# First attention's front: norms per token, a diagonal product to spread them, roots as powers on GpSimd, and first rows read by tile

## The chip, the cores and the metric

The kernel runs on one core of one Trainium2 chip, as a single launch. Its time is the device time of one execution in microseconds (us). Eleven executions of the kernel before gave a median of 2311.44 us, from 2306.51 to 2316.15. One further execution was recorded by the profiler; all profile lines come from that one.

The engines are named as in the profile: PE is TensorE (matmuls; PEld is its weight loads), DVE is VectorE, ACT is ScalarE, POOL is GpSimd, SP is SyncE, whose queue issues most DMAs.

## The reference

The input x has 2708 rows (tokens) of 256 features, with an adjacency matrix of 2708 x 2708. Four layers follow, each an attention over the graph and a feed-forward part. Only the front of the first attention is changed:

```python
def _L0_gnn_ref(features, adj, Wq, Wk):
    def _cos_normalize(x):
        n = jnp.linalg.norm(x, axis=-1, keepdims=True)
        return x / jnp.maximum(n, COS_EPS)          # COS_EPS = 1e-4
    Qn = _cos_normalize(features @ Wq.T)
    Kn = _cos_normalize(features @ Wk.T)
    raw_att = Kn @ Qn.T
    att = jnp.where(adj > 0, raw_att, NEG) * TEMP
    att = jax.nn.softmax(att, axis=1)
    prop_fea = att @ features
...
x = x + _L0_gnn_ref(_layernorm(x, axis=-1), adj, L0_gnn_Wq, L0_gnn_Wk)
```

So every token is layernormed, projected to a query and a key of 128 numbers each, both are divided by their lengths, and the scores are products of these unit vectors.

## The kernel before

The tokens lie in 22 tiles of 128 (the last holds 20) and are worked on in six chunks of 512 (the last has 148): chunk 0 is tiles 0 to 3, and so on. `K.__init__` has `load_x` (L65) read all rows, one DMA for a chunk (L72), each but the first two waiting until the one two before has landed.

`fast_l0_gnn` (L1690) computes the first attention. Its `front` (L1721) prepares one chunk:

1. `norm_chunk` (L1633): mean and variance of each tile on DVE (L1642, L1643), then 1/sqrt(variance + 1e-5) as a square root on ACT (L1645) and a reciprocal on DVE (L1646), a shift (L1647), and the scaling of the tiles into `fa`, the odd ones on ACT (L1654), the even ones on DVE (L1656).
2. Eight PE transposes (L1625) and two copies give the features by rows, `fT` (L100 on DVE, L102 on ACT).
3. Eight matmul instructions (L1732; every f32 product of this kernel appears as two) give Q and K, transposed: 128 features by 512 tokens. ACT squares each into `sq` (L1740), DVE copies each to `QT` and `KT` (L1741).
4. Norms. For Q, the squares of 128 tokens at a time are the weights against a column of ones (L1747): a column of sums with a token on each partition, `rq`, which the exponential later takes as its scale. For K the norm must lie along the free axis, in every partition: a matrix of ones times the squares (L1754) gives a 128x512 tile of sums.
5. Square roots of both on ACT (L1758, L1762), maximum with 1e-4 and reciprocal on DVE (L1767, L1768 for Q; L1770, L1771 for K, over 128x512), and on POOL the product of `KT` with the result (L1773).

Then the scores: for each chunk g of targets and each tile j of sources a step (`scores`, L1804): one product of `QT` and `KT` (L1811), Exp on ACT with the scale `rq` (L1835), the mask by the adjacency tile on DVE (L1836), and, two steps later (`sums`, L1850), four products with `fa` that accumulate (L1867). Six chunks by 22 tiles make 132 steps.

The front of chunk 0 is written ahead of the loop. The fronts of chunks 1 to 5, some rows for the last tile and weights of the next layer (`fronts`, L1781) are a generator, of which the loop takes two pieces per step during the first 22 steps. Tile j of the sources needs `QT`, `rq` and `fa` of its own chunk; the scores of chunk g need the whole `KT` of that chunk. The fronts share two PSUM tiles (`psf`, L1715).

Engines run their instructions strictly in the order of their queues. That order is made when the kernel is built: a planner simulates the program with estimated durations and gives an engine, when it is free, the earliest written instruction that is ready by the estimate. It may thus put work of a later chunk ahead of an instruction of chunk 0 that still waits. `issue_after(ins)` makes the instructions written inside it come behind `ins` on that engine's queue. The waits themselves are semaphores that the framework sets by the data.

Of the kernel before, what the change touches and what calls it, by code (L numbers as in the profile page):

```python
# [8 lines left out]
F32 = mybir.dt.float32  # L9
# [4 lines left out]
AF = mybir.ActivationFunctionType  # L14
# [31 lines left out]
class K:  # L46
# [3 lines left out]
    def __init__(self, ctx, tc, x_in):  # L50
        self.tc = tc
        self.nc = nc = tc.nc
        self.flip = 0
        pool = ctx.enter_context(tc.tile_pool(name="shared", bufs=1))
        self.x = pool.tile([128, NT, D], F32, name="x")
        nc.vector.memset(self.x[:, NT - 1, :], 0.0)
        self.load_x(lambda r: x_in[r])
        self.ident = pool.tile([128, 128], F32, name="ident")
        make_identity(nc, self.ident)
        self.ones = pool.tile([1, 128], F32, name="ones")  # L60
        nc.vector.memset(self.ones, 1.0)
        self.eps = pool.tile([128, 1], F32, name="eps")
        nc.vector.memset(self.eps, 1e-5)

    def load_x(self, src, also=None):  # L65


        ld = []
        for c0, cs in CHUNKS:
            t0, n = c0 // 128, cs // 128  # L70
            ld.append(
                self.nc.sync.dma_start(  # L72
                    self.x[:, t0 : t0 + n, :],
                    src(slice(c0, c0 + n * 128)).rearrange("(t p) d -> p t d", p=128),
                )
            )
            if cs % 128:
                ld.append(
                    self.nc.sync.dma_start(
                        self.x[:TAIL, NT - 1, :], src(slice((NT - 1) * 128, N))  # L80
                    )
                )
        for i, inst in enumerate(ld):
            if also:
                also(inst)
            if i > 1:
                self.tc.add_manual_dep(
                    inst.ins,
                    ld[i - 2].ins.name,
                    mybir.DependencyInfo(  # L90
                        mybir.DependencyClass.Sync, mybir.DependencyReason.DATA
                    ),
                    reason="the first are to land first",
                )
# [1433 lines left out]
class Fast(K):  # L1528
# [101 lines left out]
            dst = out(kk)  # L1630
            self.copy(dst, p[:, : dst.shape[-1]])

    def norm_chunk(self, pool, fa, t0, n, spare=False):  # L1633


        nc = self.nc
# [5 lines left out]
            nc.vector.bn_stats(st, self.x[:, t0 + i, :])  # L1642
            nc.vector.bn_aggr(mv[:, i, :], st)  # L1643
        yield
        nc.scalar.activation(rs[:, :n], mv[:, :n, 1], AF.Sqrt, bias=self.eps)  # L1645
        nc.vector.reciprocal(rs[:, :n], rs[:, :n])  # L1646
        nc.vector.scalar_tensor_tensor(  # L1647
            sh[:, :n], mv[:, :n, 0], -1.0, rs[:, :n], ALU.mult, ALU.mult
        )
        for i in range(n):  # L1650
            src, dst = self.x[:, t0 + i, :], fa[:, i, :]
            r, s = rs[:, i : i + 1], sh[:, i : i + 1]
            if i % 2 or spare:
                nc.scalar.activation(dst, src, AF.Identity, bias=s, scale=r)  # L1654
            else:
                nc.vector.tensor_scalar(dst, src, r, s, ALU.mult, ALU.add)  # L1656
        yield

    def logits(self, fa, fT, dst, wg, bg, E, pool):
# [30 lines left out]
def fast_l0_gnn(k, adjT, wqkT, pool_, other):  # L1690
# [7 lines left out]
    with ExitStack() as ctx:  # L1698
# [19 lines left out]
        def psum():  # L1718
            return psf.tile([128, 512], F32, name="f_ps")

        def front(c0, cs):  # L1721
            bl = blocks(c0, cs)
            t0, n = bl[0][0], len(bl)
            yield from k.norm_chunk(two, fa[:, t0:, :D], t0, n)
            fT = two.tile([128, 2, 512], F32, name="fT")
            k.transposed(fa, bl, psum, lambda kk: fT[:, kk, :cs])
            yield
# [14 lines left out]
                q.append(sq)  # L1742
            yield

            pq, pk = psum(), psum()
            for t, o, m in bl:
                nc.tensor.matmul(  # L1747
                    pq[:m, t - t0 : t - t0 + 1],
                    lhsT=q[0][:, o : o + m],
                    rhs=every[:, :1],  # L1750
                    start=True,
                    stop=True,
                )
            nc.tensor.matmul(pk[:, :cs], lhsT=every, rhs=q[1][:, :cs], start=True, stop=True)  # L1754
            for m in sorted({b[2] for b in bl}):
                ts = [b[0] for b in bl if b[2] == m]
                r = slice(ts[0], ts[-1] + 1)
                nc.scalar.activation(  # L1758
                    rq[:m, r], pq[:m, ts[0] - t0 : ts[-1] + 1 - t0], AF.Sqrt
                )  # L1760
            rk = one.tile([128, 512], F32, name="rk")
            nc.scalar.activation(rk[:, :cs], pk[:, :cs], AF.Sqrt)  # L1762
            yield
            for m in sorted({b[2] for b in bl}):
                ts = [b[0] for b in bl if b[2] == m]
                r = rq[:m, ts[0] : ts[-1] + 1]
                nc.vector.tensor_scalar(r, r, 1e-4, None, ALU.max)  # L1767
                nc.vector.reciprocal(r, r)  # L1768
            r = rk[:, :cs]
            nc.vector.tensor_scalar(r, r, 1e-4, None, ALU.max)  # L1770
            nc.vector.reciprocal(r, r)  # L1771
            kt = KT[:, c0 : c0 + cs]
            nc.gpsimd.tensor_tensor(kt, kt, r, ALU.mult)  # L1773
            yield

        def last_rows():
# [134 lines left out]
        side = fronts()  # L1911
        todo = [(g, j) for g in range(G) for j in range(NT)]
        ahead = []
        for i in range(len(todo) + 2):
            if i < len(todo):
                ahead.append(scores(*todo[i]))
# [3164 lines left out]
```

## Time and profile before

| | |
|---|---|
| median of 11 executions | 2311.44 us (2306.51 to 2316.15) |
| the profiled execution, its own time | 2316.39 us |
| its span, first to last instruction | 2314.7 us |
| mean granted PE clock | 0.954 (1.00 in the first 300 us) |
| first transpose (L1625) | 9.28 us |
| first projection (L1732) | 11.92 us |
| first score (L1811) | 26.30 us |
| first and last sum (L1867) | 30.7 and 373.9 us |
| ACT table loads of the first attention's chunk 0, from 26 to 112 us | 13, each 1283 ns |
| reciprocal over 128x512 (L1771) | 5, each 3351 ns |

The profile is read in four views. The page gives each engine's busy time and a row of 40 slices with the busy share in tenths. The view by stretches gives the busy time of each engine in a part of the span. The waits say who waited for whom, how long in total, how often, and the longest. The timeline lists instructions in order: start, duration, engine, line, operation, output <- inputs, shape, count, and in brackets the idle time before and what ended it. A duration of several merged instructions reaches from the first's start to the last's end, and a matmul's contains the time in the pipeline; how fast PE goes is read from the starts.

### The profile page before, as it was taken

To read this page: it belongs to the slowest core of one execution; us is meant where nothing else is said; L and a number is where in the kernel's file an instruction comes from. 1 tells how busy PE (TensorE), PEld (TensorE's weight loads), DVE (VectorE), ACT (ScalarE), POOL (GpSimd) and SP (SyncE) were. 2 spreads that over 40 slices of the span, in tenths; PEclk is the share of its full clock that TensorE was granted. 3 is DMA by queue.
4 is the path that set the end of the run, shared out by engine and by line. 5 is a ranking of instruction groups with operands and counts; after the bars stand their busy time and mean duration, and the time that the engine had idled before them with its cause. 6 is when DMAs were issued, how large, how long until landed. Compare 5 with 4: busy or idle time off the path is not lost. (4 is left out here: it accounts for less than half of the span.)

```text
span 2314.7 us, 31484 instructions
## 1 busy us (share of the span) xinstructions
PE 2151.8 (93%) x11216; PEld 1486.0 (64%) x11216; DVE 1491.7 (64%) x3382; ACT 694.5 (30%) x1501; POOL 477.3 (21%) x558
## 2 busy tenths in 40 slices
PE   7999999989999999999799999689999999986997
PEld 4766675568898767777578877457743333335885
DVE  7478887846695287467646563163588898872544
ACT  7556554221112222122230013023551221211221
POOL 2000002202353333664200012314110000003221
PEclk9999999979999999999899996899999999997998
DMA  5244323021497242441355544012133333415440
GB/s 151 66 112 114 110 78 113 1 78 49 142 255 216 75 117 67 100 94 22 81 160 150 143 136 98 3 40 86 49 92 97 114 115 91 123 42 183 142 144 15
DMA packets 167888, 235.28 MB, mean 102 GB/s; under 512 B 31901, under 2 KB 101251, under 8 KB 167716
## 3 DMA queue, kind: packets, MB, share of 16 engines
q1 hardware_dynamic: 112176, 154.91, 23.1%
q0 software_dynamic: 36592, 62.13, 10.8%
q10 hardware_dynamic: 18948, 16.05, 2.2%
q8 instruction: 95, 1.56, 0.3%
q14 instruction: 77, 0.63, 0.1%
HBM read 200.31 MB, written 33.22 MB: 101 GB/s over the span
## 5 line engine op out<-in xcount | busy, mean ns | idle before, releaser
L3583 DVE SCALAR_TENSOR_TENSOR PT<-Rr,Q,aj 128x512 f32<-128x512 f32 (+3 forms) x630 | 395.6, 681 | 104.9 <-PE acc_ps L3682 80.5
L3757 PE MATMUL acc_ps<-PT,V 128*64 128x512 f32 (+4 forms) x2016 | 333.7, 551 | 0.0
L3757 PEld LDWEIGHTS acc_ps<-PT,V 128*64 128x64 f32 (+1 forms) x2016 | 94.2, 123 | 210.3 <-issue 159.6
L1867 PE MATMUL acc_ps<-fa,PT 128*128 128x257 f32 x882 | 215.1, 383 | 1.2 <-DVE out L1887 1.2
L1867 PEld LDWEIGHTS acc_ps<-fa,PT 128*128 128x128 f32 x882 | 163.9, 190 | 67.3 <-issue 35.4
L3682 PE MATMUL acc_ps<-V,PT 128*128 128x257 f32 x882 | 196.6, 384 | 2.0 <-issue 1.9
L3682 PEld LDWEIGHTS acc_ps<-V,PT 128*128 128x128 f32 x882 | 167.8, 192 | 29.7 <-issue 2.8
L3340 PE MATMUL y_ps<-w2t,hT 128*128 128x256 f32 x768 | 173.6, 384 | 0.1
L3323 PE MATMUL h_ps<-xT,w1t 128*128 128x384 f32 (+2 forms) x544 | 168.7, 466 | 1.5 <-ACT hT L3330 1.3
L3340 PEld LDWEIGHTS y_ps<-w2t,hT 128*128 128x128 f32 x768 | 146.2, 193 | 20.9 <-DVE wgat L3807 0.5
L3323 PEld LDWEIGHTS h_ps<-xT,w1t 128*128 128x128 f32 x544 | 103.0, 199 | 54.3 <-ACT xT L3312 3.3
L3330 ACT ACTIVATE hT<-h_ps,b1t 128x384 f32<-128x384 f32 (+2 forms) x136 | 73.2, 539 | 179.3 <-PE h_ps L3323 176.9
L3354 POOL DMA_INDIRECT acc<-ys,ids x48 | 91.8, 1913 | 153.5 <-DVE ys L3351 104.1
L2538 PE MATMUL acc_ps<-V,at 128*128 128x258 f32 (+3 forms) x924 | 119.0, 286 | 2.3 <-DMA at<-in_adjT 1.6
L1811 PE MATMUL s_ps<-KT,QT 128*128 128x512 f32 (+1 forms) x252 | 116.4, 548 | 3.7 <-ACT PT L1835 2.3
L4784 POOL DMA_INDIRECT xe<-fd,idg x32 | 32.8, 1023 | 418.1 <-DVE ids L4754 401.9
L1836 DVE SCALAR_TENSOR_TENSOR PT<-aj,PT 128x512 f32<-128x512 int32 (+1 forms) x126 | 79.1, 632 | 56.8 <-ACT PT L1835 56.5
L2538 PEld LDWEIGHTS acc_ps<-V,at 128*128 128x128 f32 (+1 forms) x924 | 111.8, 185 | 5.5 <-DMA at<-in_adjT 2.5
L4310 PE MATMUL y_ps<-w2t,hT 128*128 128x256 f32 (+1 forms) x432 | 103.9, 390 | 6.8 <-issue 6.8
L1791 ACT ACTIVATE junk<-aj,mhalf 128x512 bf16<-128x512 int32 (+1 forms) x126 | 84.3, 669 | 77.4 <-DMA aj<-in_adjT 76.6
L3348 DVE TENSOR_TENSOR ys<-y_ps,b2t 128x256 f32<-128x256 f32 x48 | 20.3, 422 | 128.3 <-PE y_ps L3340 91.1
L4310 PEld LDWEIGHTS y_ps<-w2t,hT 128*128 128x128 f32 (+1 forms) x432 | 80.3, 191 | 24.1 <-issue 10.8
(800 smaller groups left out, 3526.3 us busy)
## 6 DMA issues: line engine op xcount, KB each, us to landing
aj<-in_adjT SPq DMA_DIRECT2D x294, 256.0 KB, 2.6
at<-in_adjT POOLq DMA_DIRECT2D x105, 256.0 KB
w1t<-in_L_ffn_W SPq DMA_DIRECT2D x8, 1024.0 KB
w2t<-in_L_ffn_W SPq DMA_DIRECT2D x8, 1024.0 KB, 6.3
w1t<-in_L_ffn_w SPq DMA_DIRECT2D x8, 1024.0 KB
w2t<-in_L_ffn_w SPq DMA_DIRECT2D x8, 1024.0 KB, 5.7
fd<-fa ACTq DMA_DIRECT2D x13, 512.0 KB, 3.3
aj<-in_adjT SPq DMA_DIRECT2D x21, 202.0 KB, 2.6
```

What stands on the lines that cost most here:

```text
L1791: nc.scalar.activation(junk, src, AF.Square, bias=k.mhalf, accum_out=dst)
L1811: nc.tensor.matmul(s[:, :cs], lhsT=QT[:, j * 128 : j * 128 + 128], rhs=KT[:, c0 : c0 + cs], start=True, stop=True,)
L1836: made[0] = nc.vector.scalar_tensor_tensor(PT[p, :n], aj[p, :n], 0.0, PT[p, :n], ALU.is_gt, ALU.mult)
L1867: nc.tensor.matmul(ac, lhsT=PT[:, o : o + n], rhs=fa[:, j, :], start=j == 0, stop=False)
L2538: nc.tensor.matmul(ac[:n, :c], lhsT=at[:, o : o + n], rhs=V[:, j, r], start=j == 0 and q == 0, stop=False, skip_group_check=True,)
L3323: nc.tensor.matmul(hp, lhsT=w1t[:, kk, m * 128 : (m + 1) * 128], rhs=self.xT[:, kk, cs], start=(kk == 0), stop=(kk == 1),)
L3340: nc.tensor.matmul(y, lhsT=self.hT[:, m, i * 128 : (i + 1) * 128], rhs=w2t[:, m, :], start=(m == 0), stop=(m == M - 1),)
L3354: add = nc.gpsimd.indirect_dma_start(out=acc, out_offset=bass.IndirectOffsetOnAxis(ap=self.ids[:, i : i + 1], axis=0), in_=ys, in_offset=None,
L3583: nc.vector.scalar_tensor_tensor(PT, R, Q, aj, ALU.max, ALU.mult)
L3682: nc.tensor.matmul(ac[:n], lhsT=PT[:, o : o + n], rhs=V[:, j, 0, :], start=(j == 0), stop=False,)
L3757: nc.tensor.matmul(w.pop("out"), **w)
L4310: last = nc.tensor.matmul(y[:n], lhsT=hT[:, m, o : o + n], rhs=wts[e][1][:, m, :], start=(m == 0), stop=(m == M - 1),)
```

## The change

- `load_x` can read chunk 0 with a DMA for each of its four tiles, and does so at the start of the kernel. The later reads wait as before for the read two before them (chunk 2 for tile 3).
- The first piece of the following fronts, the statistics of chunk 1, is taken right behind chunk 0's front and tied with `issue_after` to the last DVE instruction that normalises chunk 0.
- Where `power` is set (chunks 1 to 5), `norm_chunk` adds 1e-5 on DVE and raises to -1/2 on POOL; ACT's root and DVE's reciprocal go. Chunk 0 keeps them.
- The norms of K come as those of Q do, a column per 128 tokens with a token on each partition; both lie in one PSUM tile, eight columns. The lower bound is applied to the squared length (1e-8); then root and reciprocal (chunk 0) or a power on POOL (the others), over at most eight columns. `rq` is a copy of the first four.
- To spread K's factors along the free axis, DVE makes four diagonal blocks, the identity times the factors (128x512), and a matrix of ones times these gives them in every partition. DVE instead of POOL multiplies `KT` with that, out of PSUM.
- In chunk 0 an Exp of one column, whose result nobody reads, follows the root on ACT.

```diff
@@ -54,7 +54,7 @@
         pool = ctx.enter_context(tc.tile_pool(name="shared", bufs=1))
         self.x = pool.tile([128, NT, D], F32, name="x")
         nc.vector.memset(self.x[:, NT - 1, :], 0.0)
-        self.load_x(lambda r: x_in[r])
+        self.load_x(lambda r: x_in[r], tiles=True)
         self.ident = pool.tile([128, 128], F32, name="ident")
         make_identity(nc, self.ident)
         self.ones = pool.tile([1, 128], F32, name="ones")
@@ -62,12 +62,21 @@
         self.eps = pool.tile([128, 1], F32, name="eps")
         nc.vector.memset(self.eps, 1e-5)
-    def load_x(self, src, also=None):
-        ld = []
+    def load_x(self, src, also=None, tiles=False):
+        ld, free = [], 2
         for c0, cs in CHUNKS:
             t0, n = c0 // 128, cs // 128
+            if tiles and c0 == 0:
+                for t in range(n):
+                    ld.append(
+                        self.nc.sync.dma_start(
+                            self.x[:, t, :], src(slice(t * 128, t * 128 + 128))
+                        )
+                    )
+                free = n + 1
+                continue
             ld.append(
                 self.nc.sync.dma_start(
                     self.x[:, t0 : t0 + n, :],
@@ -83,7 +92,7 @@
         for i, inst in enumerate(ld):
             if also:
                 also(inst)
-            if i > 1:
+            if i >= free:
                 self.tc.add_manual_dep(
                     inst.ins,
                     ld[i - 2].ins.name,
@@ -1630,7 +1639,7 @@
             dst = out(kk)
             self.copy(dst, p[:, : dst.shape[-1]])
-    def norm_chunk(self, pool, fa, t0, n, spare=False):
+    def norm_chunk(self, pool, fa, t0, n, spare=False, power=False):
         nc = self.nc
@@ -1642,8 +1651,13 @@
             nc.vector.bn_stats(st, self.x[:, t0 + i, :])
             nc.vector.bn_aggr(mv[:, i, :], st)
         yield
-        nc.scalar.activation(rs[:, :n], mv[:, :n, 1], AF.Sqrt, bias=self.eps)
-        nc.vector.reciprocal(rs[:, :n], rs[:, :n])
+        if power:
+            nc.vector.tensor_scalar(rs[:, :n], mv[:, :n, 1], 1e-5, None, ALU.add)
+            half = self.mhalf.to_broadcast([128, n])
+            nc.gpsimd.tensor_tensor(rs[:, :n], rs[:, :n], half, ALU.pow)
+        else:
+            nc.scalar.activation(rs[:, :n], mv[:, :n, 1], AF.Sqrt, bias=self.eps)
+            nc.vector.reciprocal(rs[:, :n], rs[:, :n])
         nc.vector.scalar_tensor_tensor(
             sh[:, :n], mv[:, :n, 0], -1.0, rs[:, :n], ALU.mult, ALU.mult
         )
@@ -1653,7 +1667,9 @@
             if i % 2 or spare:
                 nc.scalar.activation(dst, src, AF.Identity, bias=s, scale=r)
             else:
-                nc.vector.tensor_scalar(dst, src, r, s, ALU.mult, ALU.add)
+                self.normed = nc.vector.tensor_scalar(
+                    dst, src, r, s, ALU.mult, ALU.add
+                )
         yield
     def logits(self, fa, fT, dst, wg, bg, E, pool):
@@ -1721,7 +1737,7 @@
         def front(c0, cs):
             bl = blocks(c0, cs)
             t0, n = bl[0][0], len(bl)
-            yield from k.norm_chunk(two, fa[:, t0:, :D], t0, n)
+            yield from k.norm_chunk(two, fa[:, t0:, :D], t0, n, power=c0 > 0)
             fT = two.tile([128, 2, 512], F32, name="fT")
             k.transposed(fa, bl, psum, lambda kk: fT[:, kk, :cs])
             yield
@@ -1742,35 +1758,58 @@
                 q.append(sq)
             yield
-            pq, pk = psum(), psum()
-            for t, o, m in bl:
+            pn = psum()
+            for s in (1, 0):
+                for t, o, m in bl:
+                    nc.tensor.matmul(
+                        pn[:m, 4 * s + t - t0 : 4 * s + t - t0 + 1],
+                        lhsT=q[s][:, o : o + m],
+                        rhs=every[:, :1],
+                        start=True,
+                        stop=True,
+                    )
+            rn = two.tile([128, 2, 4], F32, name="rn")
+            for m in sorted({b[2] for b in bl}):
+                ts = [b[0] - t0 for b in bl if b[2] == m]
+                r = slice(ts[0], ts[-1] + 1)
+                v = rn[:m, :, r]
+                nc.vector.tensor_scalar(
+                    v,
+                    pn[:m, :8].rearrange("p (s t) -> p s t", s=2)[:, :, r],
+                    1e-8,
+                    None,
+                    ALU.max,
+                )
+                if c0 == 0:
+                    nc.scalar.activation(v, v, AF.Sqrt)
+                    nc.vector.reciprocal(v, v)
+                else:
+                    half = k.mhalf[:m, :, None].to_broadcast([m, 2, len(ts)])
+                    nc.gpsimd.tensor_tensor(v, v, half, ALU.pow)
+                nc.vector.tensor_copy(rq[:m, t0 + r.start : t0 + r.stop], v[:, 0, :])
+            if c0 == 0:
+                nc.scalar.activation(rn[:, 0, 0:1], rn[:, 0, 0:1], AF.Exp, scale=0.0)
+            yield
+            dg = one.tile([128, 4, 128], F32, name="dg")
+            pk = psum()
+            for m in sorted({b[2] for b in bl}, reverse=True):
+                ts = [b[0] - t0 for b in bl if b[2] == m]
+                r, n = slice(ts[0], ts[-1] + 1), len(ts)
+                nc.vector.tensor_tensor(
+                    dg[:m, r, :m],
+                    k.ident[:m, None, :m].to_broadcast([m, n, m]),
+                    rn[:m, 1, r, None].to_broadcast([m, n, m]),
+                    ALU.mult,
+                )
                 nc.tensor.matmul(
-                    pq[:m, t - t0 : t - t0 + 1],
-                    lhsT=q[0][:, o : o + m],
-                    rhs=every[:, :1],
+                    pk[:, r.start * 128 : r.start * 128 + n * m],
+                    lhsT=every[:m, :],
+                    rhs=dg[:m, r, :m],
                     start=True,
                     stop=True,
                 )
-            nc.tensor.matmul(pk[:, :cs], lhsT=every, rhs=q[1][:, :cs], start=True, stop=True)
-            for m in sorted({b[2] for b in bl}):
-                ts = [b[0] for b in bl if b[2] == m]
-                r = slice(ts[0], ts[-1] + 1)
-                nc.scalar.activation(
-                    rq[:m, r], pq[:m, ts[0] - t0 : ts[-1] + 1 - t0], AF.Sqrt
-                )
-            rk = one.tile([128, 512], F32, name="rk")
-            nc.scalar.activation(rk[:, :cs], pk[:, :cs], AF.Sqrt)
-            yield
-            for m in sorted({b[2] for b in bl}):
-                ts = [b[0] for b in bl if b[2] == m]
-                r = rq[:m, ts[0] : ts[-1] + 1]
-                nc.vector.tensor_scalar(r, r, 1e-4, None, ALU.max)
-                nc.vector.reciprocal(r, r)
-            r = rk[:, :cs]
-            nc.vector.tensor_scalar(r, r, 1e-4, None, ALU.max)
-            nc.vector.reciprocal(r, r)
             kt = KT[:, c0 : c0 + cs]
-            nc.gpsimd.tensor_tensor(kt, kt, r, ALU.mult)
+            nc.vector.tensor_tensor(kt, kt, pk[:, :cs], ALU.mult)
             yield
         def last_rows():
@@ -1911,6 +1950,8 @@
         side = fronts()
         todo = [(g, j) for g in range(G) for j in range(NT)]
         ahead = []
+        with tc.issue_after(k.normed.ins):
+            next(side)
         for i in range(len(todo) + 2):
             if i < len(todo):
                 ahead.append(scores(*todo[i]))
```

## The prediction

> **What bounds the kernel now.** First the page: how busy TensorE is over the span, and how its share runs from slice to slice.
>
> ```profile
> PE 2151.8 (93%) x11216; PEld 1486.0 (64%) x11216; DVE 1491.7 (64%) x3382; ACT 694.5 (30%) x1501; POOL 477.3 (21%) x558
> PE   7999999989999999999799999689999999986997
> ```
>
> PE is busy nearly everywhere, and the change touches only the start. So I split the start into two stretches (busy time of PE, PEld, DVE, ACT and POOL, granted clock, DMA share, GB/s), cut where the first score matmul begins, and then asked which waits PE has behind that cut (total, times, longest).
>
> ```profile
> 0.00:26.30 26.30, 14.12 (x42) 7.40 (x42) 20.33 (x70) 15.60 (x35) 6.57 (x26) 1.00 0.86 249
> 26.30:90.00 63.70, 63.70 (x268) 43.47 (x268) 40.24 (x67) 49.63 (x88) 11.14 (x14) 1.00 0.24 66
> ```
> ```profile
> PE s_ps L1811 <- POOL KT L1773: 1.4, 1, 1.4
> ```
>
> Before 26.30, PE works 14.12 us and otherwise waits; from 26.30 to 112 that one wait, which ends at the cut, is all it has. A busy PE can still be slow, so I checked the spacing on the timeline (start, us, engine, line):
>
> ```profile
> 46.85 0.95 PE L1747 MATMUL f_ps<-every,sq 128*128 128x1 f32 x8
> 47.66 0.68 PE L1867 MATMUL acc_ps<-fa,PT 128*128 128x257 f32 x2
> 48.17 1.02 PE L1754 MATMUL f_ps<-sq,every 128*128 128x512 f32 x2
> 49.03 1.02 PE L1811 MATMUL s_ps<-KT,QT 128*128 128x512 f32 x2
> ```
>
> Each matmul is two instructions; the next group starts 0.81 us after eight of L1747, 0.86 after two with 512 columns, and elsewhere 1.72 after eight of L1867. Nothing lies between. **Behind 26.30 the first attention is bound by PE's queue: time changes there only by PE instructions added or taken away. Before 26.30 it is bound by one chain**, on the timeline:
>
> ```profile
> 0.80 1.00 SPq L72 DMA_DIRECT2D x<-in_x  x2
> 4.72 0.75 DVE L1642 BATCH_NORM_STATS2 ln_st<-x 128x6 f32<-128x256 f32 x2 [3.24 <-DMA x<-in_x]
> 6.59 0.30 ACT L1645 ACTIVATE ln_rs<-ln_mv,eps 128x4 f32<-128x4 f32 x1 [4.51 <-DVE ln_mv L1643]
> 8.21 0.14 DVE L1646 RECIPROCAL ln_rs<-ln_rs 128x4 f32<-128x4 f32 x1
> 8.76 0.71 DVE L1656 TENSOR_SCALAR fa<-x,ln_rs,ln_sh 128x256 f32<-128x256 f32 x2
> 9.28 1.94 PE L1625 MATMUL f_ps<-ident,fa 128*128 128x128 f32 x8 [9.28 <-DVE fa L1656]
> 11.18 0.69 DVE L100 COPY fT<-f_ps 128x512 f32<-128x512 f32 x1
> 11.92 5.65 PE L1732 MATMUL f_ps<-fT,wqk 128*128 128x512 f32 x8 [0.70 <-DVE fT L100]
> ...
> 21.55 3.35 DVE L1771 RECIPROCAL rk<-rk 128x512 f32<-128x512 f32 x1
> ...
> 24.98 1.26 POOL L1773 TENSOR_TENSOR KT<-KT,rk 128x512 f32<-128x512 f32 x1 [18.94 <-DVE rk L1771]
> ...
> 26.30 1.98 PE L1811 MATMUL s_ps<-KT,QT 128*128 128x512 f32 x4 [1.42 <-POOL KT L1773]
> ```
>
> **The change, part by part.** A gain is time by which the first score comes earlier.
>
> *A. Rows by tile, layernorm first.* SP spends 0.50 us on an issue (two in 1.00). The fourth tile's is issued at 0.80 + 3 x 0.50 = 2.30. Landing: the only x transfer with a recorded time took 5.4 us, the 256 KB adjacency tiles a median of 2.6; a 128 KB tile at the head of the queue is nearest to the latter, so 2.30 + 2.7 = 5.0 (at worst 7.7). Its statistics (0.41 + 0.17) end at 5.6 instead of 6.56: 0.95. Then ACT's root is ready at 6.89, yet the reciprocal starts at 8.21, since chunk 1's statistics stand in DVE's queue; they now come behind: 1.3. Chunk 1's reciprocal (0.18) goes from ahead of L1656 too. Sum 2.4, at worst -0.25. On SP, chunk 1's rows and the weights move back by 1.5 us (wqk from 1.84 to some 3.3). At some 0.37 MB/us (the DMA view's rate from 3 us on), 1.25 MB lands near 6.5, before the projections want it. Chunk 2's issue waits for tile 3 (5.0) as it waited for chunk 0 (4.71); the adjacency issues are queued behind it, but the first scores are far off.
>
> *B. Copy of fT.* DVE started it at 11.18, behind chunk 1's work, when its four transposes (half of L1625's 1.94) had ended near 10.4. The statistics of chunk 1 now stand there: 0 to 0.8, I take 0.4. The projections keep 5.65.
>
> *C. Projections to score.* Now 17.57 to 26.30, 8.73. The chain's own rows: square 0.60, product 1.12, root 0.57, max 0.42, reciprocal 3.35, multiply 1.26, plus 0.4 of hand-overs = 7.7, so 1.0 is queueing. After: square 0.60, K's norms 0.95 (a row like L1747), max 0.17, root 0.17, reciprocal 0.18, copy 0.15, diagonal 0.69 (a 128x512 TENSOR_TENSOR on DVE, L2307), product 1.12, multiply 0.69, hand-overs 0.4 = 5.1, and the same queueing: 6.1. Gain 2.6 (1.6 with twice the queueing, 3.6 with none). The Exp table now loads behind the root, beside diagonal and product.
>
> Sum of A to C: 5.4; the first score at 20.9.
>
> *D. What PE did while it waited.* Between 19.6 and 24.9 PE did chunk 1's transposes (0.87) and projections (3.43): 4.3 us that count later if they no longer fit. The new 6.1 us hold 16 norm instructions (1.62) and the product (0.86); 3.6 are free. I let 2.6 be used: 1.7 goes behind the first score (0.7 to 4.3). PE's idle time falls by 5.4 - 1.7 = 3.7.
>
> *E. Added PE work.* Per chunk, the norms of both Q and K take 16 of the L1747 kind instead of 8; the spreading product is as long as the old one. Eight are 0.81 us. Chunk 0's are in C; chunks 1 to 4 add 4 x 0.81, chunk 5 four of them, 0.35. With 0.2 for the split product of chunk 5 and a change of shape: **3.8 us on a queue that is never idle**.
>
> *F. Roots on GpSimd.* Four to eight elements per partition; no power is in the trace. The nearest POOL rows: 0.25 us (L1800, one column) below, 1.58 (the 128x512 multiply) above. By size it is near the first; I take 0.4. Eleven of them, off PE, in one queue with the DMAs for the last rows (L1575), which at 47.8 us had waited 7.5 for `fa`: a power written behind them would wait too, but those are written behind the fronts. But the product's matmul now stands in PE's queue behind norms, max, power, copy and diagonal, placed by the planner's estimate; PE had no such wait. I allow 0.2 for each of five: 1.0 (0 to 5 x 1.58 = 7.9). Likewise DVE's shift instruction waits for the power with copies and masks queued behind it, and PE's sums wait for the masks; DVE was already shut for 3.35 us by each L1771 without PE waiting, so this is covered for chunks 2 to 5, and in chunk 0's shadow costs up to 1.2.
>
> *G. At nothing:* 13 table loads after 26.3 (13 x 1.28 = 16.7 us of ACT), DVE's four long reciprocals (4 x 3.35 = 13.4, for which it takes on 4 x 1.4 of diagonal and multiply), POOL's multiplies. PE, full at the time, hides them; if it were not, a score step would gain the ACT time that stood ahead of its Exp.
>
> Sum: -3.7 + 3.8 + 1.0 = **+1.1 us**. On the profiled execution (2316.39, span 2314.7) that is 2317.5; that execution lies 4.95 above the median, so I predict 2311.44 + 1.1 = **2312.5**.
>
> Two rules of the Trainium skill point elsewhere. The trace puts a table load at 1.28 us with the next ACTIVATE 0.02 behind it. "ScalarE: Activation LUTs", What ACT_TABLE_LOAD costs, adds a drain of 1380 ns to 1283, so 13 switches would free 35 us of ACT; the trace shows no drain, and PE waits for none of it: by the trace 0. On POOL the first multiply (1.26) was no longer than the later ones (1.58). "GPSIMD Engine Reference", Instruction dispatch, states that the first call to a freshly loaded kernel pays an IRAM load of about 6 us; if the power were such a call, the sum would be +7.
>
> **Rivals.**
>
> *Even trade* (0.54): the sum above, 2308 to 2316.
>
> *A new wait on PE* (0.22), slower: each spreading product stands at the head of PE's queue until a power that takes as long as the longest POOL arithmetic row, 1.58, has come through. Five times 1.58 instead of 1.0 in all adds 6.9, chunk 0's shadow 1.2: 2320.6. It decides once the five waits pass 0.9 us each (4.5 - 1.0 = 3.5 above the forecast, +4.6 in all). For it: PE is in order and full. Against: PE has four to eight sums per step that the planner can put in between.
>
> *All covers hold* (0.16), faster: A at 2.9 (a tile lands in 2.25, since 128 KB less take 0.35 at 0.37 MB/us), B 0.8, C 3.6, the transition of the matmul spacing from 0.86 to 0.43 (seen at 16.1) early enough to spare five instructions 0.43 each, 2.1, chunk 1 delayed by only 0.7, F 0: 2.9 + 0.8 + 3.6 + 2.1 - 0.7 - 3.8 = 4.9 faster, 2306.5.
>
> *The rows do not come earlier* (0.08): four issues cost SP 1.5 us, and the last tile lands as late as the 5.4 row says; A gives -0.25 instead of 2.4: 2315.2.
>
> **Numbers.** A measurement of this kernel can tell 0.2% (4.6 us) from no change. Even trade and late rows stay within it, the new wait lies beyond on the slow side, the covers on the fast side; a planner that orders everything anew can throw a few us to either side. Faster 0.17, same 0.60, slower 0.23. The range, 2305 to 2321, reaches to both outer cases.
>
> **What would show it.** A: first L1625 transposes near 6.9 (was 9.28). C: first L1811 near 20.9. E: 16 instead of 8 norm matmuls per chunk, 0.81 apart. D and F: PE waits behind the first score, none before; waits on DVE's diagonal or on a POOL power would make the slow rival true. I am wrong if the first attention's end moves by more than 4 us against its start, or if later stages differ.

## The result and the profile after

The kernel after took 2329.32 us (median of 14 executions, 2327.45 to 2337.29); beside it the kernel before took 2312.84 (53 executions). The ratio is 1.0076, 95% interval 1.0066 to 1.0086: **slower by some 16.5 us, where +1.1 was forecast and the range ended at 2321.** The profiled execution took 2330.86, its span is 2329.1, 14.4 more than before.

The page of the kernel after: TensorE's totals, its busy share by slices, and the row of its granted clock.

```profile
PE 2163.7 (93%) x11262; PEld 1492.6 (64%) x11262; DVE 1477.4 (63%) x3384; ACT 674.3 (29%) x1473; POOL 481.9 (21%) x563
PE   7999999989999899999799998799999999986997
PEclk9999999988999899999889996899999999997998
```

PE is busy 11.9 us longer with only 46 more instructions: some of them ran slowly. The page cannot say where, so here is the view by stretches (busy time of PE, PEld, DVE, ACT, POOL; clock, DMA share, GB/s), cut at the first score and with two short windows.

```profile
0.00:27.27 27.27, 12.59 (x39) 6.94 (x39) 16.81 (x67) 12.71 (x27) 8.31 (x27) 0.93 0.86 241
27.27:90.00 62.73, 58.81 (x239) 37.95 (x239) 24.99 (x55) 26.07 (x52) 11.05 (x11) 0.97 0.19 52
26.00:28.00 2.00, 2.00 (x6) 1.16 (x5) 1.31 (x3) 0.09 (x1) 0.00 (x0) 0.50 0.03 10
110.00:112.00 2.00, 2.00 (x6) 1.57 (x5) 0.00 (x0) 0.02 (x1) 0.00 (x0) 0.50 0.00 0
```

The first score starts at 27.27, not at 20.9, so the front gained nothing. Behind it PE, which was busy for all 63.70 us before, now stands still for 62.73 - 58.81 = 3.92 of them; and in two places it runs at half its clock. The waits from the first score to the end of target chunk 0 name what it stands still for (total, times, longest):

```profile
DVE rq L1789 <- POOL rn L1788: 8.2, 6, 1.8
PE f_ps L1804 <- DVE dg L1798: 4.5, 5, 1.0
```

PE waits five times for the diagonal, DVE before it for the power. One of these waits on PE's timeline, from a chunk's norms to its product, and the power on POOL that belongs to it:

```profile
49.68 1.93 PE L1764 MATMUL f_ps<-every,sq 128*128 128x1 f32 x16
51.47 1.11 PE L1906 MATMUL acc_ps<-fa,PT 128*128 128x257 f32 x4
52.42 1.02 PE L1850 MATMUL s_ps<-KT,QT 128*128 128x512 f32 x2
54.42 1.12 PE L1804 MATMUL f_ps<-dg,every 128*128 128x512 f32 x2 [0.97 <-DVE dg L1798]
```
```profile
51.90 1.67 POOL L1788 TENSOR_TENSOR rn<-rn,mhalf 128x8 f32<-128x8 f32 x1 [11.55 <-DVE rn L1776]
```

Sixteen norm instructions take 1.79 us (49.68 to 51.47), where eight took 0.81 before. The planner put 1.8 us of sums and scores between norms and product, but from the score's start to the product 2.00 us pass instead of 0.86: the power alone lasts 1.67, and with maximum, copy and diagonal around it DVE and POOL need 2.7 (51.65 to 54.36). The groups of POOL show the price of a power by columns (the last number before the idle time is the mean in ns):

```profile
L1788 POOL TENSOR_TENSOR rn<-rn,mhalf 128x8 f32<-128x8 f32 x4 | 7.0, 1748 | 41.5 <-DVE rn L1776 41.5
L1657 POOL TENSOR_TENSOR ln_rs<-ln_rs,mhalf 128x2 f32<-128x2 f32 x1 | 0.7, 696 | 3.1 <-DVE ln_rs L1655 3.1
```

It grows with the columns: 0.70 for two, 1.02 for four, 1.75 for eight; the prediction took 0.4. The front of chunk 0, on the timeline, answers to the chain shown of before:

```profile
6.49 0.43 DVE L1651 BATCH_NORM_STATS2 ln_st<-x 128x6 f32<-128x256 f32 x1 [1.76 <-DMA x<-in_x]
...
8.47 1.94 PE L1634 MATMUL f_ps<-ident,fa 128*128 128x128 f32 x8 [8.47 <-DVE fa L1670]
...
11.38 0.43 DVE L1651 BATCH_NORM_STATS2 ln_st<-x 128x6 f32<-128x256 f32 x1 [0.99 <-DMA x<-in_x]
11.73 0.67 DVE L109 COPY fT<-f_ps 128x512 f32<-128x512 f32 x1
...
12.46 5.84 PE L1748 MATMUL f_ps<-fT,wqk 128*128 128x512 f32 x8 [2.04 <-DVE fT L109]
...
21.27 0.21 ACT L1784 ACTIVATE rn<-rn 128x8 f32<-128x8 f32 x1 [0.33 <-DVE rn L1776]
...
22.03 1.01 POOL L1657 TENSOR_TENSOR ln_rs<-ln_rs,mhalf 128x4 f32<-128x4 f32 x1 [6.21 <-ACT fa L1668]
23.07 0.16 DVE L1661 SCALAR_TENSOR_TENSOR ln_sh<-ln_mv,ln_rs 128x4 f32<-128x4 f32 x1 [0.89 <-POOL ln_rs L1657]
23.15 0.20 DVE L1785 RECIPROCAL rn<-rn 128x8 f32<-128x8 f32 x1
...
24.41 2.07 PE L1804 MATMUL f_ps<-dg,every 128*128 128x512 f32 x2 [3.38 <-DVE dg L1798]
```

Three things hold it. The fourth tile's statistics waited until 6.49. The copy of `fT` stood behind a statistics instruction of chunk 2, which waited 0.99 for its rows; their read was issued only when the fourth tile had landed, at 6.49 instead of 4.71 before. And chunk 0's reciprocal, whose root was done at 21.48, stood behind a shift (L1661) of a later chunk that waited for that chunk's power. Then PE, idle for 3.38, did the spreading product at half clock: 1.87 us from its start to the next (26.28) instead of 0.86.

**The ledger.** I cut at the first instruction for the last source tile of target chunk 0, in the kernel before and in the kernel after; the difference is +18.39.

```profile
112.52 0.72 PE L1861 MATMUL acc_ps<-fat,PT 32*128 32x257 f32 x8
130.91 0.72 PE L1900 MATMUL acc_ps<-fat,PT 32*128 32x257 f32 x8
```

| term | forecast | measured | from |
|---|---|---|---|
| first score | -5.4 | +1.0 | 26.30 -> 27.27 |
| chunk 1's PE work displaced behind it | +1.7 | +3.9 | 4 transposes 0.43, 8 projections 3.44 |
| norms and split product | +3.8 | +4.8 | 4 x 0.98 + 0.45, split 0.4 |
| waits for the diagonal | +1.0 | +5.35 | five gaps 1.09, 1.14, 1.17, 1.16, 0.79 above the normal spacing |
| PE at half clock behind the first score | 0 | +3.4 | 1.65 behind 27.27, 1.72 behind 108.76 |

The five gaps exceed the 4.5 of the waits by what the hand-over costs each time. From there on both kernels do the same work: the last sums come 17 us later (391.0 against 373.9), and the two spans end 14.4 apart. The 2.7 between these lie behind the first attention, where nothing was changed; single executions of the kernel before alone differ by up to 17 (2304.70 to 2321.58).

### The profile page after: what moved, and what is told of

It reads as the page before. It is cut to its first block, busy times and chain, and to the rows that moved or that the text cites. A ratio compares the mean times of both kernels' runs of the same rounds, so it can differ in the third digit from the quotient of the medians.

```text
span 2329.1 us, 31566 instructions
## 1 busy us (share of the span) xinstructions
PE 2163.7 (93%) x11262; PEld 1492.6 (64%) x11262; DVE 1477.4 (63%) x3384; ACT 674.3 (29%) x1473; POOL 481.9 (21%) x563
## 5 line engine op out<-in xcount | busy, mean ns | idle before, releaser
L1874 ACT ACTIVATE PT<-s_ps,rq 128x512 f32<-128x512 f32 (+1 forms) x126 | 78.5, 627 | 79.8 <-PE s_ps L1850 77.1
```

What stands on the lines that cost most here:

```text
L1874: nc.scalar.activation(PT[p, :n], s[p, :n], AF.Exp, scale=r)
```

## The experiments

*Theory:* PE is full behind the first score, so what is added to its queue counts in full (norms, chunk 1's displaced work), and the powers on POOL put five new waits on it; the earlier start did not come since in-order queues hold chunk 0's instructions behind others that wait for a DMA or a power. *Rivals:* the new front of chunk 0, or the reading by tile alone, is the loss and the powers are covered; or the chain norms - diagonal - product stalls PE whatever takes the root.

The kernels ran on three chips: e1 to e4 on one where before took 2284.86 us, e5 to e8 on one with 2283.76, e9 to e11 on one with 2311.93. Ratios are to before on the same chip; times inside the start are compared directly. "End" is the cut of the ledger, "stretch" the time from first score to end.

| kernel | transposes | projections | first score | end | stretch | ratio to before |
|---|---|---|---|---|---|---|
| before | 9.28 | 11.92 | 26.30 | 112.52 | 86.22 | |
| after | 8.47 | 12.46 | 27.27 | 130.91 | 103.64 | 1.0076 [1.0066, 1.0086] |
| e1 rows and order | 7.05 | 11.78 | 27.09 | 117.56 | 90.47 | 1.0028 [1.0013, 1.0043] |
| e2 no power for the norms | 7.06 | 12.91 | 27.7 | 123.6 | 95.9 | not read |
| e3 chunk 0 alone | 8.00 | 12.47 | 25.91 | 122.58 | 96.67 | 1.0045 [1.0027, 1.0064] |
| e4 after, whole read | 7.98 | 10.00 | 23.30 | 124.31 | 101.0 | 1.0047 [1.0032, 1.0062] |
| e5 order alone | 7.90 | 9.93 | 26.95 | 115.83 | 88.88 | 1.0003 [0.9990, 1.0015] |
| e6 more norm instructions | 9.24 | 12.14 | 26.68 | 116.79 | 90.11 | 1.0027 [1.0013, 1.0042] |
| e7 chunk 0, gated | 7.84 | 9.87 | 25.29 | 116.00 | 90.71 | 1.0013 [0.9998, 1.0027] |
| e8 after again | 7.09 | 12.11 | 26.92 | 130.64 | 103.72 | 1.0074 [1.0050, 1.0099] |
| e9 e7, checks gated too | 7.91 | 9.93 | 21.41 | 111.80 | 90.39 | 1.0010 [0.9994, 1.0025] |
| e10 roots for powers | 7.14 | 12.36 | 26.30 | 122.27 | 95.97 | 1.0038 [1.0022, 1.0054] |
| e11 old norms, gated | 7.89 | 9.91 | 23.50 | 114.86 | 91.36 | 0.9987 [0.9969, 1.0006] |

### The powers: e2 and e10

e2 puts a reciprocal on DVE in the place of the norms' power in chunks 1 to 5 (no root is taken there, so the scores have other values); the statistics' powers stay.

```diff
-                    nc.vector.reciprocal(v, v)
-                else:
-                    half = k.mhalf[:m, :, None].to_broadcast([m, 2, len(ts)])
-                    nc.gpsimd.tensor_tensor(v, v, half, ALU.pow)
+                nc.vector.reciprocal(v, v)
```

> The changed kernel with the power of the norms left out in chunks 1 to 5: a reciprocal of the bounded squares on DVE stands in its place, so the norms are not roots there. The layernorm's powers stay. Theory (PE waits for the diagonal because the power takes 1.7 us and the planner takes it for less): the five waits of PE for the diagonal after the first score, 5.3 us of gaps in all, fall under 1 us, time 4 to 6 us less than the changed kernel, near 2324 against 2329. Rival (the wait is the longer chain of DVE and PE itself, or is laid out anew wherever it fits): the gaps stay above 3 us, time within 2 us of the changed kernel.

Its whole time, 12619 us, says nothing: the other values made the kernel's general path run afterwards. In the stretch that the experiment is about, the five waits for the diagonal are gone, and it lasts 95.9 instead of 103.64. PE's order is that of after, with the same 1.8 us between norms and product (50.54 to 52.35), but from the maximum to the diagonal's end only 1.2 us pass (50.72 to 51.92) instead of 2.7. e10 gives ACT the root and DVE the reciprocal, for norms and statistics, in all chunks, and computes the same as the changed kernel:

```diff
-                if c0 == 0:
-                    nc.scalar.activation(v, v, AF.Sqrt)
-                    nc.vector.reciprocal(v, v)
-                else:
-                    half = k.mhalf[:m, :, None].to_broadcast([m, 2, len(ts)])
-                    nc.gpsimd.tensor_tensor(v, v, half, ALU.pow)
+                nc.scalar.activation(v, v, AF.Sqrt)
+                nc.vector.reciprocal(v, v)
...
-            yield from k.norm_chunk(two, fa[:, t0:, :D], t0, n, power=c0 > 0)
+            yield from k.norm_chunk(two, fa[:, t0:, :D], t0, n)
```

> The changed kernel with both GpSimd powers replaced by ScalarE's square root and VectorE's reciprocal of the same small tiles in chunks 1 to 5; everything else as changed. Theory (the power's own 0.7 to 1.75 us on GpSimd, in the chain norms - max - power - diagonal - product, stalls PE): PE's five waits for the diagonal, 5.35 us together in the changed kernel, fall below 1 us, the stretch from the first score to the end of target chunk 0 falls from 103.7 to 97 to 98, ratio 1.0045 to 1.005 instead of 1.0074. Rival (the chain stalls PE whatever takes the root, since it now has a diagonal and its table loads on ScalarE come back): waits stay at 1 us each, ratio stays at 1.0074.

Among e10's waits behind the first score, only these two concern the chain of the norms, and PE has none at all:

```profile
DVE rn L1776 <- PE f_ps L1764: 6.5, 5, 1.6
DVE rn L1784 <- ACT rn L1783: 2.1, 4, 0.7
```

DVE waits at most 0.7 us for ACT, where it waited up to 1.8 for POOL. The stretch is 95.97, 7.7 less than after, and the ratio 1.0038: about half of the loss. Of the 7.7, the waits are 5.35; the rest is the stretch at half clock near 110 (1.7) and less of the one behind the first score. But e10 does not show that ACT's root is quicker than the power. In chunk 2 its chain is nearly as long as after's, since a table load stands in it:

```profile
51.12 1.55 PE L1902 MATMUL acc_ps<-fa,PT 128*128 128x257 f32 x6
51.27 1.28 ACT L1783 ACT_TABLE_LOAD   x1
51.29 0.17 DVE L1776 TENSOR_SCALAR rn<-f_ps 128x8 f32<-128x8 f32 x1 [1.31 <-PE f_ps L1764]
53.13 0.68 DVE L1794 TENSOR_TENSOR dg<-ident,rn 128x512 f32<-128x512 f32 x1
55.95 1.02 PE L1800 MATMUL f_ps<-dg,every 128*128 128x512 f32 x2
```

From the maximum to the diagonal's end it takes 2.5 us (51.29 to 53.81), but the planner put 4.8 us of PE's work in between (51.12 to 55.95), in other chunks 2.7 to 4.8, where with the power it put 1.4 to 2.2. So what stalls PE is the difference between the chain and what the planner puts beside it. With the power the chain is too long for its place, as e2 shows in the same order; whether the planner takes the power for shorter than it is, and whether PE would wait for roots in after's order, no run shows.

### Added PE instructions: e6

The kernel before, with eight more norm instructions per chunk (four for the last) into columns that nobody reads:

```diff
+            if c0:
+                for t, o, m in bl:
+                    nc.tensor.matmul(
+                        pq[:m, t - t0 + 8 : t - t0 + 9],
+                        lhsT=q[0][:, o : o + m],
+                        rhs=every[:, :1],
+                        start=True,
+                        stop=True,
+                    )
```

> The kernel before, with the norm matmuls of Q in chunks 1 to 5 issued twice, the second time into columns that nobody reads: only PE work is added, 8 instructions a chunk. Theory (PE's queue is never idle behind the first score): 4 x 0.81 + 0.35 = 3.6 us later at the last sum of target chunk 0 (116.1 instead of 112.5), time +3.6 us (0.16%). Rival (such short matmuls fit into gaps of a queue that is only nominally busy): below +1 us.

The timeline of e6: from 47.98 to 48.79 and from there to 49.69, 0.81 and 0.90 for eight each, none hidden.

```profile
47.98 0.95 PE L1747 MATMUL f_ps<-every,sq 128*128 128x1 f32 x8
48.79 1.03 PE L1756 MATMUL f_ps<-every,sq 128*128 128x1 f32 x8
49.69 0.68 PE L1876 MATMUL acc_ps<-fa,PT 128*128 128x257 f32 x2
```

The end comes 4.3 later than before's, the ratio is 1.0027 (3 to 10 us). PE's queue is the bound there, as the prediction had it.

### Rows, order, chunk 0: e1, e5, e3, e4, e8

e1 is the kernel before with the change's `load_x` and the early, tied statistics; e5 has the latter alone, chunk 0 read whole:

```diff
+        with tc.issue_after(k.normed.ins):
+            next(side)
...
-        self.load_x(lambda r: x_in[r])
+        self.load_x(lambda r: x_in[r], tiles=True)
```

> The kernel before with two parts of the change alone: chunk 0 read by tile, and chunk 1's statistics tied behind chunk 0's normalising. Norms and roots as before. Theory (the front gained nothing, because the fourth tile lands at 6.5 us against 4.7 for the whole chunk, and because the statistics that went behind now stand ahead of the copy of fT): first transposes near 8.5 us instead of 9.28, first projections near 12.4 instead of 11.92, first score near 26.8 instead of 26.30, time +0.5 us (0 to +2). Rival (the prediction's part A and B, the gain being lost only later, to the new norms): first score near 23.5, time 2 to 3 us faster than before.

> The kernel before with one part of the change: chunk 1's statistics tied behind chunk 0's normalising; chunk 0 read whole, norms, roots and multiply as before. Theory (an earlier first score is worth only what PE's idle time before it falls by, since PE is full behind it): first projections near 10.0 us as in the whole-read run, first score near 24.5 instead of 26.30, but chunk 1's transposes and projections (4.3 us) partly behind it; last sum of target chunk 0 at 111 to 114 instead of 112.5, time within 2 us of before. Rival (the earlier score is passed on whole): last sum near 110.7, time 1.8 us faster.

e1's time missed its expectation (6.8 us more than before, 0 to 2 expected), and so did its transposes. With tiles, these start at 7.05, near the 6.9 of the prediction, and in e5 without them at 7.90. But the copy that follows is late with tiles. DVE in e1:

```profile
10.71 0.43 DVE L1651 BATCH_NORM_STATS2 ln_st<-x 128x6 f32<-128x256 f32 x1 [1.53 <-DMA x<-in_x]
11.05 0.67 DVE L109 COPY fT<-f_ps 128x512 f32<-128x512 f32 x1
```

A statistics instruction of chunk 2, written behind it but planned ahead of it, waits for its rows, and the copy behind that. In e5 the copy starts at 9.20 and the projections at 9.93, 1.85 us before e1's. So the reading by tile, which gains 0.85 at the transposes, loses 1.85 at the projections. Of the 5.0 by which e1's end is late, 0.8 are the first score and some 3.4 PE at half clock (1.7 behind the first score, where 0.51 was granted, and 1.7 behind 95.4). In e5, too, the first score is late (26.95, expected 24.5): PE's product for the norms of K waited 2.66 us for ACT, whose queue held a check of an adjacency tile (a Square that only sums, one per tile) that waited for its DMA.

e3 has the changed kernel's norms, diagonal and product in chunk 0 only, with rows and order as changed, and the old norms in the other chunks; e4 is the changed kernel with chunk 0 read whole; e8 is the changed kernel itself.

```diff
+            if c0 == 0:
...
+                return
             pq, pk = psum(), psum()
```

> The change in chunk 0 only: rows by tile, statistics order, the diagonal, the early Exp table; chunks 1 to 5 have the roots, norms and multiply of before. Theory (of the 17.4 us that the first score to the end of the first target chunk takes longer, added norm matmuls and waits for the diagonal are 9.8 us and come from chunks 1 to 5 alone): these are gone, time 2313 to 2318, that is 0 to 5 above before, depending on how much of chunk 1 PE does before the first score. Rival (chunk 0's front, with the slow PE clock after it, is the main loss): time above 2320.

> The changed kernel with chunk 0 read by one DMA, as before; all else changed. Theory (four DMAs land later than one): chunk 0's statistics end near 6.56 us instead of 7.14, first transposes near 7.9 instead of 8.47, first score 0.5 to 1 us earlier than 27.27; time 0 to 1.5 us less than the changed kernel. Rival (reading by tile is a gain that later parts eat up): first transposes later than 8.47, time up to 2 us more than the changed kernel.

> The changed kernel again, on the chip of these runs. Theory: last sum of target chunk 0 near 128 to 131 us, five waits of PE for the diagonal of 0.8 to 1.2 us each, ratio 1.0066 to 1.0086 as measured elsewhere. Rival (a part of the loss was that execution's own: rows that landed late, the PE clock at half in two stretches): last sum nearer to 124 and ratio nearer to 1.005.

e3 keeps 1.0045 with no power in it, 8.3 us where its theory allowed 0 to 5; its rival, more than 7 us lost by chunk 0's front and the slow clock after it, describes it. The new front moves chunk 1's PE work (3.9) behind the first score and brings that score only 0.4 earlier. Its stretch also holds waits for `fT` (1.2) and for `QT` behind a 3.35 us reciprocal (0.85), and half clock costs it some 3.8 us, 3.4 of them near 99. e4 shows most sharply that an earlier first score is not yet a faster kernel: 23.30, 3.0 before the old kernel's, and still 1.0047, with the five waits as in after. Its end is 6.6 before after's, more than expected: 4.0 by the first score, the rest by less half clock. The ratios, 1.0047 against 1.0076, were taken on two chips, but their intervals lie apart: with the order of the queues that this kernel has, the reading by tile is a loss. e8 repeats after's ratio, waits and half-clock stretches, so these do not belong to one execution alone.

### What holds chunk 0's front: e7, e9, e11

e7, meant to beat both kernels, has e3's front, chunk 0 read whole, and the statistics of chunks 2 to 5 tied behind chunk 0's multiply. e9 also ties ACT's adjacency checks for the first target chunk behind chunk 0's root:

```diff
-            yield from k.norm_chunk(two, fa[:, t0:, :D], t0, n)
+            piece = k.norm_chunk(two, fa[:, t0:, :D], t0, n)
+            if t0 > 4:
+                with tc.issue_after(gate[0].ins):
+                    next(piece)
+                yield
+            yield from piece
...
+                if g == 0 and gate[1]:
+                    with tc.issue_after(gate[1].ins):
+                        check(aj[:, :cs], cs, chk[:, g, j : j + 1])
```

> A version meant to beat both: the diagonal norms in chunk 0 alone, chunk 0 read whole, roots and norms of chunks 1 to 5 as before, and the statistics of chunks 2 to 5 tied behind chunk 0's key multiply on DVE, so that DVE serves chunks 0 and 1 first and PE has chunk 1's transposes and projections to do before the first score. Theory: first score 22 to 23 us, chunk 1's projections before it, last sum of target chunk 0 at 108 to 112 instead of 112.5, time 0 to 4 us faster than before. Rival (chunk 1 still comes behind the first score, as in the run with chunk 0 alone): last sum at 114 or later, time at least 2 us slower than before.

> As e7_gate, and ScalarE's adjacency checks for the first target chunk (an ACT Square per adjacency tile) are tied behind chunk 0's root and table load, so that none that waits for its DMA stands ahead of K's square. Theory (in-order ACT queue blocked by DMA-waiting checks delayed chunk 0): the 2.45 us wait of the check and PE's 3.41 us wait for K's square go, first score 25.3 -> about 22; if that earliness is worth its size, the last source row of target chunk 0 comes at about 113 instead of 116.0 and the ratio is about 0.9998. Rival (PE is full behind the first score and what it leaves undone counts later): the first score comes near 22 all the same, but the end of target chunk 0 stays at 115 to 117, ratio 1.001 as e7_gate.

e7 did not reach what was expected of it: first score 25.29, end 116.00. Its ACT shows what stands ahead of K's square (the second line), and PE waited 3.41 us for that square:

```profile
16.75 0.72 ACT L1870 ACTIVATE junk<-aj,mhalf 128x512 bf16<-128x512 int32 x1 [2.45 <-DMA aj<-in_adjT]
...
17.47 0.58 ACT L1763 ACTIVATE sq<-f_ps 128x512 f32<-128x512 f32 x1
```

With the checks behind, e9's PE:

```profile
9.93 4.46 PE L1755 MATMUL f_ps<-fT,wqk 128*128 128x512 f32 x8
15.08 1.95 PE L1772 MATMUL f_ps<-every,sq 128*128 128x1 f32 x16 [0.69 <-ACT sq L1763]
18.56 2.07 PE L1812 MATMUL f_ps<-dg,every 128*128 128x512 f32 x2 [1.53 <-DVE dg L1806]
20.43 1.06 PE L1634 MATMUL f_ps<-ident,fa 128*128 128x128 f32 x4
21.41 1.27 PE L1890 MATMUL s_ps<-KT,QT 128*128 128x512 f32 x2
22.52 0.60 PE L1634 MATMUL f_ps<-ident,fa 128*128 128x128 f32 x4
22.96 1.02 PE L1890 MATMUL s_ps<-KT,QT 128*128 128x512 f32 x2
23.82 3.60 PE L1755 MATMUL f_ps<-fT,wqk 128*128 128x512 f32 x8
```

The first score is at 21.41: the 20.9 of the prediction is nearly had, once nothing that waits for a DMA stands in the front's queues. From e7 to e9 the end moved by 4.2 for 3.9 at the first score, so earliness is worth its size when the work behind it stays the same, as e9's theory had it (the ratio, 1.0013 and 1.0010, does not resolve this). Against before it does not: 4.9 earlier at the score, 0.7 at the end, since half of chunk 1's transposes and all of its projections (last lines) now lie behind. The whole time cannot be told from before's.

e11 keeps the old norms everywhere, with e9's two gates and the early statistics.

> The kernel before with the statistics order of the change (e5_order), the statistics of chunks 2 to 5 tied behind chunk 0's KT multiply and the adjacency checks of the first target chunk tied behind chunk 0's root of K; old norms everywhere. Theory (checks that wait for DMAs held ScalarE): PE's 2.66 us wait before chunk 0's spreading product goes, first score 26.95 -> about 24.3, end of target chunk 0 115.8 -> 113 to 114, ratio 0.999 to 1.000. Rival (earliness is not worth its size behind a full PE): the first score at about 24.3 but the end of target chunk 0 stays near 116, ratio 1.000 to 1.001.

First score 23.50, 2.8 before the old kernel's, and chunk 1's projections done ahead of it (18.16), so nothing is displaced; yet the end, 114.86, is 2.3 later than before's (113 to 114 was expected). PE then waits for `fT` (two waits, 1.6 together) and loses clock as here:

```profile
87.38 4.60 PE L2318 MATMUL f_ps<-wsl,wx 64*128 64x64 f32 x32
91.92 3.79 PE L1883 MATMUL acc_ps<-fa,PT 128*128 128x257 f32 x8
95.50 1.76 PE L1822 MATMUL s_ps<-KT,QT 128*128 128x512 f32 x2
```

The 32 small matmuls take 4.54 instead of the 3.71 of after, the eight sums 3.58 instead of 1.72, the score 1.69 instead of 0.86: 3.5, which with the waits makes the 5.1 us by which the stretch is longer than before's. The ratio, 0.9987 [0.9969, 1.0006], holds no change: no version here is shown faster than before.

## Why the prediction was wrong

What bounds the kernel was read rightly: PE's queue behind the first score (e6, e9), one chain before it. At the end of target chunk 0 the sum was +1.1 and the measured difference +18.4, 17.3 apart: A to C 6.4, F 4.3, PE's clock 3.4, D 2.2, E 1.0. The step that failed most in the sum is the gain of A to C (5.4 earlier forecast, 1.0 later measured), and the one that failed in judgement is F.

- **F, the powers: mis-sized by mechanism and number.** "I allow 0.2 for each of five: 1.0" became 5.35, since a power takes 1.75 us on eight columns and not 0.4. The row chosen as nearest "by size" (0.25, one column) was the wrong one; the upper bound taken from the 1.58 row was close to the truth. The rival "a new wait on PE" described what happened: its point was 0.9 us a wait, and the gaps are 0.79 to 1.17. It had 0.22 and should have had more. Against it the prediction put the four to eight sums per step that the planner can place in between; in after it placed 1.4 to 2.2 us of work there, too little. e2 and e10 take the waits away, 7.7 us with the clock's part. F also named the shift that waits for a power in DVE's queue; it held chunk 0's reciprocal for 0.89.
- **A, rows: the start right, the use wrong.** The transposes came at 7.05 to 7.14 in e1, e2, e8 and e10, as forecast (6.9); in e3 (8.00) and in the profiled execution of after (8.47) the fourth tile came later. The later issue of chunk 2's rows, which the prediction named and put at nothing, matters in B.
- **B, the copy of `fT`: the failing assumption of the front.** I put 0 to 0.8 us of chunk 1's statistics ahead of it as a gain of 0.4. In fact a statistics instruction of chunk 2 that waits for its DMA stands there: from transposes to projections 3.99 us instead of the 2.24 I had counted on. Nor do the projections keep their 5.65: they took 4.46 to 5.48 where they follow the transposes at once (e4, e5, e7, e9, e11) and 5.48 to 6.61 behind a gap.
- **C, projections to score: right as a chain, wrong as a queue.** Forecast 6.1; e9, with the gates, takes 7.0 from the projections' end (14.39) to 21.41, of which 1.0 is the product at half clock. After took 8.97, with the DVE wait and PE's half clock.
- **D: 1.7, measured 3.9**, inside its bounds of 0.7 to 4.3. The planner took all of the projections and half of the transposes out of the idle time instead of the part that no longer fitted.
- **E: right**, 4.4 and 0.4 against 3.8 (16 instructions cost 0.98 more than 8, not 0.81).
- **Missing:** PE's clock. The prediction counted PE's work behind the first score at full clock; 3.4 us there came from half clock.

The terms measured sum to +18.4 at the end of target chunk 0; the range left no room for F's upper bound and a lost front together.

## What to carry to other kernels

An operation that moves to an idle engine is not free when the bounding engine waits for its result in order: price one call by its own row or leave the whole range open, and compare the whole chain with what the planner does put in between, not with what it could. An earlier start counts only less the work that the bound engine did while it waited. In strictly ordered queues, look what the planner lets stand ahead of the first chain, above all instructions that wait for a DMA: a gate on those (e7 to e9: 3.9 us) did more for the first score here than the reading by tile, though no whole time was shown faster for it.

## What the runs showed of the hardware

- **PE's clock.** After an idle time of 3.38 us (after) the product and the next four microseconds ran at a granted 0.50; in e9 idle times of 0.69 and 1.53 with only one-column matmuls between them were enough (0.50 granted from 18.56 to 21.41). The Trainium skill, "TensorE: Matmul & The Clock Gate", Part 1, has the array fall to half rate after an idle window of some 3.4 us; the first case agrees, the second would fit if so little work counts as idle, which no run isolates.
- **The granted clock at a kernel's start.** It reads 1.00 over the first transposes and projections, in the kernel before too, yet eight transposes last 1.94 us there (9.28 before, 8.47 after) and 1.04 later (35.92 before, 57.97 after). A mean of 1.00 over the first 300 us of before hides this.
- **Half clock without idleness.** A run of 32 matmuls of 64x64 (3.7 to 4.5 us) came with half clock in six records: in after, e1, e5 and e8 for some 3.4 us, from about the end of the run on, in e3 and e11 for some 6.8, twice as long, beginning inside it (estimates from the granted clock; in e1 0.52 over 3.52 us). The same run in e2, e4, e7, e9 and e10 was at full clock and followed by full clock, and so were two runs of 16 in before and e6. In after:

```profile
105.05 3.78 PE L2341 MATMUL f_ps<-wsl,wx 64*128 64x64 f32 x32
108.76 3.64 PE L1906 MATMUL acc_ps<-fa,PT 128*128 128x257 f32 x8
112.20 1.11 PE L1850 MATMUL s_ps<-KT,QT 128*128 128x512 f32 x2
```

The eight sums take 3.44 (108.76 to 112.20) with PE busy throughout. That a run of small matmuls counts as little work would fit, and where the run falls in a window could decide; no run here changes that alone, so the cause stays open. So 1.7 to 3.4 us of a difference between two kernels of this case can be such a stretch alone.

- **A power on POOL** costs 0.70, 1.02 and 1.75 us for two, four and eight f32 columns over 128 partitions. The first one in the kernel after lasted 1.05 and the next 1.01 (four columns each): the load of some 6 us on the first call to a freshly loaded kernel, of which the Trainium skill, "GPSIMD Engine Reference", Instruction dispatch, speaks and which the prediction weighed, is not seen.
